# One attention block per pair of graphs in a two-layer graph network: fewer visits to the half-width column tiles of TensorE

## The chip, the core and the metric

The kernel runs on one core of a Trainium2 chip, in float32 throughout. The metric is the time of one execution in microseconds (us), the median of several runs. The core has five engines with an instruction queue each: TensorE (PE in the profile, with its weight loads apart as PEld), VectorE (DVE), ScalarE (ACT), GpSimd (POOL) and SyncE (SP), which only issues DMAs here. TensorE writes to PSUM, which has eight banks of 512 float32 values per partition; the other operands lie in SBUF.

## What is computed

The input is x, 128 graphs of 128 nodes with 512 features, and adj, a 0/1 adjacency for each graph. Two layers follow each other, each with a residual and a normalization over the features:

```python
# layer 0: attention with 8 heads of 64 features
feats = einsum('bnf,hfu->bhnu', X, W)
dense = leaky_relu(e_self[..., :, None] + e_neigh[..., None, :], 0.2) + NEG_BIG * (1 - A)
out   = relu(concat_heads(softmax(dense) @ feats) + b)
x     = layernorm(x + out)
# layer 1: two hypergraph convolutions with the same 128x128 operator R of the graph
h = layer_norm(relu(R @ (x @ W1.T) + b1))          # 1024 features
y = R @ (h @ W2.T) + b2                            # 512 features
x = layernorm(x + (y + x))
```

The softmax is divided out at the end: the heads' features carry a 65th column of ones, so a product of the exponentials with them gives the sum of a row beside its 64 results.

## The kernel before

Graphs are worked on in 64 pairs. Each pair passes through stages that lie in five successive *slots* of the schedule (the lags 0 to 4). In one slot, every stage runs once, each for another pair: while pair p has its attention (lag 2), pair p-1 is in its two convolutions (lag 3), and pair p+1 gets its features (lag 1). The kernel lists all stages with a lag and a time inside the slot, sorts by `time + (p + lag) * T` with T = 38.6, and emits the instructions in this order. The times are thus places in an order, not measured times; each engine then executes its own part of the list strictly in order and waits where data is missing. `at(lag, time, fn, ...)` and `@step(lag, time)` enter a stage; `since` and `until` limit it to some pairs. A few pairs at the start and the last one have an order of their own (`first`, `LAST`).

Products of a pair that share weights are built from seven products with sums of operands in place of eight (`chain`): "pf" for the features of layer 0, "ph" for the first convolution, "py" for the second. A chain takes three PSUM banks, X, Y and W. The product numbered 1 opens bank X, a ScalarE copy (L332) takes the bank's contents away, then products 6, 7 and 4 add to it, with further copies between. GpSimd makes the operand sums ahead of it (`x_sums` and `h_sums` at L458, `z_sums` at L785), VectorE or ScalarE add up the results (`f_sum` L499, `h_sum` L812, `y_sum` L881).

The attention, lag 2:
- exponentials are written to DRAM and read back in blocks, and transposed on VectorE (`e_transpose` L630) into `eT`;
- `attend` (L667) multiplies, for a graph g and a half q of its heads, each head's 128x128 exponentials with its 128x65 features, in two parts of 64 output rows. A part uses half of TensorE's columns, a column tile, and two such parts can be in the array together. Each call takes a PSUM bank (`pav`); both calls of graph 0 lie together, and both of graph 1 some 5 us later, with a feature product and the first "py" product between;
- `attended` (L681, L682, VectorE) divides by the 65th column into `y`;
- `add_bias` (L691, GpSimd), `residual` (L698, VectorE; relu and adding x), `moments` (L706, L707, VectorE), `rstds` (L712 VectorE, L714 GpSimd; the result is rsa), then `first_shift` and `first_output` (L732, L739, ScalarE) finish the normalization.

In the next slot `propagate` (L762, TensorE) multiplies the finished `y` with R into the banks pz, `z_evict` (L774, ScalarE) copies these to zT, and the "ph" chain starts on zT (L797) while GpSimd makes its sums zS (L785). Later in the slot, ScalarE squares h, GpSimd folds the squares (`squares` L850, three levels per graph), and `sum_blocks` (L896 to L901, VectorE) reduces them for the variance; the rest goes over DRAM (`write_sums`, `read_sums`).

PSUM banks are handed out in turn: the ninth request gets the first bank again, once all who read it are done.

Of the kernel before, what the change touches and what calls it, by code (L numbers as in the profile page):

```python
# [8 lines left out]
F32 = mybir.dt.float32  # L9
AF = mybir.ActivationFunctionType  # L10
ALU = mybir.AluOpType
# [9 lines left out]
def kernel(  # L21
# [45 lines left out]
    nc = tc.nc  # L67
    G, N, F = x.shape
    P = 128
    DH = w1t.shape[1]  # L70
    H = 8
    U = F // H
# [11 lines left out]
    work = ctx.enter_context(tc.tile_pool(name="work", bufs=1))  # L84
    small = ctx.enter_context(tc.tile_pool(name="small", bufs=4))
# [3 lines left out]
    def bank(name):  # L89
        return psum.tile([P, HALF], F32, tag="bank", name=name)  # L90
# [109 lines left out]
    for i in range(2):  # L200
        t = const.tile([P, 2, H, UW + 1], F32, name=f"ft{i}")
# [99 lines left out]
    LAST = PAIRS - 1  # L301
    steps = []

    def step(lag, time, since=0, until=PAIRS):

        def keep(fn):
            steps.append((lag, time, fn.__name__, range(since, until), fn, ()))
            return fn
        return keep

    def at(lag, time, fn, *args, since=0, until=PAIRS):
        steps.append((lag, time, fn.__name__, range(since, until), fn, args))

    def chain(kind, lag, times, multiply, w, extra=0, since=0, until=PAIRS):

        tag = "chain" if w == HALF else "half"  # L320

        def product(p, s, i):
            where, start = {1: ("X", 1), 2: ("Y", 1), 6: ("X", 0), 5: ("W", 1), 7: ("X", 0),
                            4: ("X", 0), 3: ("W", 0)}[i]
            if start:
                s[kind, where] = bank(f"{kind}{where}_{p}")
            multiply(s, i, s[kind, where], start)

        def copy(p, s, i):
            n = w + (extra if i < 2 else 0)  # L330
            t = s[kind, i] = work.tile([P, HALF if w == HALF else FW], F32, tag=f"{tag}_{i}", name=f"{kind}{i}_{p}")
            nc.scalar.copy(t[:, :n], s[kind, "X"][:, :n])  # L332

        for i, t in zip((1, 2, 6, 5, 7, 4, 3), times):
            at(lag, t, product, i, since=since, until=until)
        for i, t in enumerate(times[7:]):
            at(lag, t, copy, i, since=since, until=until)
# [145 lines left out]
    def feature(s, i, to, start):  # L483
# [4 lines left out]
          feature, FW, since=2)  # L488
# [181 lines left out]
                )  # L670

    for (g, q), t in (((0, 0), 20.65), ((0, 1), 20.7), ((1, 0), 25.95), ((1, 1), 26.8)):
        at(2, t, attend, g, q)

    def attended(p, s, g):
        if g == 0:
# [7 lines left out]
                t[:, :, :U], rden[:, q, :].unsqueeze(2).to_broadcast([P, HH, U]), op=ALU.mult,  # L684
            )

    at(2, 22.5, attended, 0)
    at(2, 27.9, attended, 1)

    def add_bias(p, s, g):  # L690
        nc.gpsimd.tensor_tensor(s["y"][:, g, :], s["y"][:, g, :], b0_bc, op=ALU.add)  # L691

    at(2, 24.1, add_bias, 0)
    at(2, 29.2, add_bias, 1)

    def residual(p, s, g):
        y = s["y"][:, g, :]
# [21 lines left out]
            op1=ALU.mult,  # L719
        )  # L720

    at(2, 26.2, residual, 0)
    at(2, 30.7, residual, 1)
    at(2, 30.8, rstds, "a")

# [140 lines left out]
    def weigh(s, i, to, start):  # L866
        rows_product(s, i, halves(s["h"], KH // 2), s["hS"], w2_sb, QU, KH // 2, 1, to, start)

    chain("py", 3, (24.2, 29.4, 27.7, 32.9, 31.2, 35.35, 37.1, 26.2, 29.6, 33.1), weigh,
          QU, 1, until=LAST)  # L870

    def y_sum(p, s, g, j, i, where):
# [16 lines left out]

    @step(3, 30.3, until=LAST - 1)
    def sum_blocks(p, s):

        t = s["sq"][:, :, 1, :].rearrange("p g (c f) -> p g c f", c=NB)
        nc.vector.transpose(t, s["sq"][:, :, 0, :].rearrange("p g (c n) -> p g c n", c=NB))  # L896
        nc.vector.tensor_reduce(
            sums_in[:, :2 * NB].rearrange("p (c g) -> p g c", g=2), t, AX.X, ALU.add
        )
        s["sr"] = work.tile([P, B], F32, tag="sr", name=f"sr_{p}")  # L900
        nc.vector.transpose(s["sr"], sums_in)  # L901

    @step(3, 30.32, until=LAST - 1)
    def write_sums(p, s):
        s["sd"] = dram.tile([NB, B, B], F32, tag="sd", name=f"sd_{p}")
        nc.sync.dma_start(s["sd"].rearrange("b q n -> (b q) n"), s["sr"])
# [311 lines left out]
```

## Time and profile before

| | |
|---|---|
| time, median of 3 runs | 2462.02 us (2461.99 to 2462.17) |
| span of the profiled run | 2459.7 us, TensorE clock 0.997 of full |
| busy: PE, PEld | 2427.1 us (99%), 2149.0 us (87%) |
| busy: DVE, ACT, POOL | 2023.0 us (82%), 1532.1 us (62%), 1828.1 us (74%) |
| attention products (L667), 4096 matmuls | 147.9 us busy |
| VectorE's division (L682), 256 | 108.6 us busy, 424 ns each |
| GpSimd's bias (L691), 128 | 162.9 us busy, 1273 ns each |
| GpSimd's squares (L850), 384 | 343.5 us busy, 895 ns each on average |
| VectorE's residual (L698), 128 | 154.4 us busy, 1206 ns each on average |

"Busy" counts an engine's instructions as they lie in time; an instruction that is held up inside the engine counts as busy too, so a mean can hide two kinds of durations. The program writes a float32 matmul as two instructions, which is why 4096 matmuls stand for 2048 products. The page's part 4 follows the work that ended last back through the program, at each step to what released it; the "waits" list names who waited for whom; the "timeline" shows an engine's instructions in order with start and duration, and in brackets the idle time before one.

### The profile page before, as it was taken

How to read it: one execution, taken by the hardware profiler on the slowest of the kernel's cores; microseconds unless marked ns; L12 is line 12 of the kernel's file. 1: busy time of each engine (PE TensorE's matmuls, PEld its weight loads, DVE VectorE, ACT ScalarE, POOL GpSimd, SP SyncE). 2: the span in 40 equal slices, each digit the busy share in tenths (PEclk: the TensorE clock that was granted, in tenths of full speed). 3: DMA queues.
4: the chain of work that ended last, by engine and by line, in shares of the span. 5: the costliest groups of instructions: out<-in, count | busy, mean ns of one | idle time of the engine just before them, and what ended most of it. 6: DMA issues, size and time to landing. Idle time of an engine off the chain costs nothing.

```text
span 2459.7 us, 53018 instructions
## 1 busy us (share of the span) xinstructions
PE 2427.1 (99%) x18273; PEld 2149.0 (87%) x18273; DVE 2023.0 (82%) x4580; ACT 1532.1 (62%) x4481; POOL 1828.1 (74%) x2060
## 2 busy tenths in 40 slices
PE   7999999999999999999999999999999999999998
PEld 5888888888888888888888888888888888888897
DVE  7988888888888888888888888888888888888876
ACT  4665665765756656657557566566575675665763
POOL 5877777777787777777777777778778777777774
PEclk9999999999999999999999999999999999999999
DMA  6545445445455454454454554554545545545531
GB/s 183 143 140 145 145 133 156 141 131 152 138 139 145 141 144 145 132 156 140 129 152 139 143 145 143 146 144 129 153 141 132 152 139 143 143 141 147 145 110 52
DMA packets 432763, 345.30 MB, mean 140 GB/s; under 512 B 153176, under 2 KB 382064, under 8 KB 432496
## 3 DMA queue, kind: packets, MB, share of 16 engines
q1 hardware_dynamic: 429024, 337.46, 48.5%
q10 hardware_dynamic: 3472, 4.47, 0.6%
q8 instruction: 145, 2.38, 0.4%
q14 instruction: 122, 1.00, 0.1%
HBM read 239.08 MB, written 102.73 MB: 139 GB/s over the span
## 4 chain that ended last, share of the span: by engine, by line
PE 50%; DVE 19%; POOL 19%; ACT 6%; issue 3%; DMA 2%; SPq 0%; POOLq 0%; ACTq 0%; DVEq 0%
PE phX L797 10%; PE pyX L476 9%; POOL hS L458 6%; PE pfX L476 5%; PE phW L797 5%; PE pyW L476 5%; POOL zS L785 4%; POOL sq L850 3%; ACT nb L595 3%; PE pav L667 3%; DVE y L953 3%; PE pz L762 2%; PE phY L797 2%; PE pq L963 2%; PE pfW L476 2%
## 5 line engine op out<-in xcount | busy, mean ns | idle before, releaser
L797 PEld LDWEIGHTS phX<-zS,w_sb 128*128 128x128 f32 x3072 | 363.1, 192 | 32.4 <-issue 31.0
L332 ACT COPY py<-pyX 128x257 f32<-128x257 f32 x189 | 70.7, 374 | 506.9 <-PE pyX L476 504.3
L797 PE MATMUL phX<-zS,w_sb 128*128 128x128 f32 x3072 | 374.3, 275 | 1.7 <-POOL xS L458 1.2
L850 POOL TENSOR_TENSOR sq<-sq 128x512 f32<-128x512 f32 (+2 forms) x384 | 343.5, 895 | 20.1
L579 POOL TENSOR_TENSOR nb<-nb,neg 128x512 f32<-128x512 f32 x256 | 318.7, 1279 | 7.6 <-DMA nb<-rd 7.6
L609 ACT ACTIVATE nb<-nb,nm 128x128 f32<-128x128 f32 x1024 | 317.6, 391 | 8.3 <-DVE nm L601 8.3
L595 ACT ACTIVATE nb<-nb,ft 128x128 f32<-128x128 f32 x1020 | 317.2, 389 | 7.5 <-POOL nb L579 7.5
L714 POOL TENSOR_TENSOR rso<-veo,mhalf 128x2 f32<-128x2 f32 x63 | 44.2, 702 | 371.2 <-DVE veo L712 371.2
L827 ACT ACTIVATE h<-h,vecs 128x128 f32<-128x128 f32 x768 | 245.0, 392 | 54.9 <-DVE h L812 54.9
L601 DVE TENSOR_REDUCE nm<-nb 128x4 f32<-128x512 f32 x256 | 174.6, 683 | 111.4 <-ACT nb L595 98.3
L476 PE MATMUL pyX<-w_sb,hS 128*128 128x257 f32 x1008 | 245.6, 385 | 0.0
L476 PE MATMUL pyX<-w_sb,h 128*128 128x257 f32 x1008 | 239.4, 379 | 0.5 <-ACT py L332 0.5
L476 PE MATMUL pyW<-w_sb,hS 128*128 128x256 f32 x1008 | 238.6, 378 | 1.0 <-DVE y L881 1.0
L476 PEld LDWEIGHTS pyW<-w_sb,hS 128*128 128x128 f32 x1008 | 190.7, 189 | 28.7 <-POOL rsa L714 1.4
L476 PEld LDWEIGHTS pyX<-w_sb,hS 128*128 128x128 f32 x1008 | 185.7, 189 | 28.7
L476 PEld LDWEIGHTS pyX<-w_sb,h 128*128 128x128 f32 x1008 | 186.4, 190 | 25.5 <-ACT py L332 0.9
L691 POOL TENSOR_TENSOR y<-y,b_bc 128x512 f32<-128x512 f32 x128 | 162.9, 1273 | 60.4 <-DVE y L682 60.4
L698 DVE SCALAR_TENSOR_TENSOR y<-y,x 128x512 f32<-128x512 f32 x128 | 154.4, 1206 | 56.8 <-POOL y L691 55.1
L667 PEld LDWEIGHTS pav<-ft,eT 128*64 128x64 f32 x4096 | 130.0, 137 | 44.3 <-issue 41.9
L953 DVE SCALAR_TENSOR_TENSOR y<-y,rsh,bw_bc 128x512 f32<-128x512 f32 x126 | 148.6, 1218 | 21.1 <-POOL rsh L949 18.1
L630 DVE STREAM_TRANSPOSE eT<-eb 128x512 f32<-128x512 f32 x252 | 163.5, 687 | 0.9 <-DMA eb<-ed 0.8
L838 ACT ACTIVATE sq<-h 128x512 f32<-128x512 f32 x256 | 160.6, 628 | 2.1
(174 smaller groups left out, 5750.5 us busy)
## 6 DMA issues: line engine op xcount, KB each, us to landing
nb<-rd SPq DMA_DIRECT2D x127, 512.0 KB
ed<-nb SPq DMA_DIRECT2D x126, 512.0 KB
eb<-ed SPq DMA_DIRECT2D x504, 128.0 KB
x<-in_x_dram SPq DMA_DIRECT2D x64, 512.0 KB
out_dram<-o SPq DMA_DIRECT2D x63, 512.0 KB
xb<-in_x_dram SPq DMA_DIRECT2D x248, 128.0 KB
a<-in_adj_dram SPq DMA_DIRECT2D x64, 128.0 KB
w<-in_adj_dram SPq DMA_DIRECT2D x128, 64.0 KB
```

The lines of the kernel that those rows point to most:

```text
L476: nc.tensor.matmul(to[:, :n], lhs[:, k, :], rhs[:, k, :n], start=bool(start) and k == 0, stop=(k == nk - 1), skip_group_check=True,)
L579: nc.gpsimd.tensor_tensor(t, t, neg[:, :, None, :].to_broadcast([P, NB, HH, B]), op=ALU.add)
L595: nc.scalar.activation(t, t, AF.Prelu, bias=s["ft"][:, g, h, 0:1], alpha=SLOPE)
L601: nc.vector.tensor_reduce(s["nm"][:, g, hs], scores(p, s, g, hs).rearrange("p b h j -> p h b j"), AX.XY, ALU.max, negate=True,)
L609: nc.scalar.activation(t, t, AF.Exp, bias=s["nm"][:, g, h:h + 1])
L630: nc.vector.transpose(s["eT"][:, g, hs, :].rearrange("p h (b i) -> p h b i", b=NB), s["eb", g][:, :, hs, :].rearrange("p b h j -> p h b j"),)
L667: nc.tensor.matmul(t[rows, h * (U + 1):(h + 1) * (U + 1)], s["eT"][:, g, q * HH + h, rows], s["ft"][:, g, q * HH + h, 2:], start=True, sto ...
L691: nc.gpsimd.tensor_tensor(s["y"][:, g, :], s["y"][:, g, :], b0_bc, op=ALU.add)
L797: nc.tensor.matmul(to[:, m * N:(m + 1) * N], w[:, k, m * P:(m + 1) * P], rhs[:, k, :], start=bool(start) and m == 0 and k == 0, stop=(k == ...
L827: nc.scalar.activation(dst[:, k, :], src[:, k, :], AF.Relu, bias=b1_sb[:, c:c + 1])
L850: nc.gpsimd.tensor_tensor(t[:, :n, :], t[:, :n, :], t[:, n:2 * n, :], op=ALU.add)
L953: nc.vector.scalar_tensor_tensor(t, t, s["rs", "h"][:, g:g + 1], bw_bc.rearrange("p (j c) -> p j c", j=2), op0=ALU.mult, op1=ALU.add,)
```

## The change

From pair 1 to the last but one, the four `attend` calls become one block that holds both graphs. It uses three banks: seven heads of graph 0, seven heads of graph 1 (7 x 65 = 455 columns each), and one bank for the eighth head of both. The division is done in three steps in place of four, the shared bank first. The block stands at 24.1, where the first "py" product stood; that product moves ahead to 21.0 and its copy to 23.0. The bank of the eighth heads is taken at 20.9, ahead of that product. What follows the attention moves too: on GpSimd, the bias of graph 0 goes from 24.1 to 28.05, which is behind the squares of graph 1 (26.0, 27.3, 28.0), and the bias of graph 1 right behind it to 28.1; on VectorE, graph 0's residual goes from 26.2 to 29.0, and `sum_blocks` from 30.3 to 28.9. The purpose is that TensorE changes to the half-width tiles and back once for a pair instead of twice. The first and the last pair keep the old form.

```diff
-        at(2, t, attend, g, q)
+        at(2, t, attend, g, q, until=1)
+        at(2, t, attend, g, q, since=LAST)
+
+    HB = H - 1
+
+    @step(2, 20.9, since=1, until=LAST)
+    def attend_rest(p, s):
+        s["pav", 2] = bank(f"pav_{p}_2")
+
+    @step(2, 24.1, since=1, until=LAST)
+    def attend_pair(p, s):
+
+        rest = s["pav", 2][:, :2 * (U + 1)].rearrange("p (g u) -> p g u", g=2)
+        to = [(rest[:, g, :], g, HB) for g in range(2)]
+        for g in range(2):
+            t = s["pav", g] = bank(f"pav_{p}_{g}")
+            to += [(t[:, h * (U + 1):(h + 1) * (U + 1)], g, h) for h in range(HB)]
+        for t, g, h in to:
+            for c in range(2):
+                rows = slice(c * P // 2, (c + 1) * P // 2)
+                nc.tensor.matmul(
+                    t[rows], s["eT"][:, g, h, rows], s["ft"][:, g, h, 2:], start=True, stop=True,
+                )
...
-    at(2, 22.5, attended, 0)
-    at(2, 27.9, attended, 1)
+    for g, t in enumerate((22.5, 27.9)):
+        at(2, t, attended, g, until=1)
+        at(2, t, attended, g, since=LAST)
+
+    @step(2, 26.3, since=1, until=LAST)
+    def attended_pair(p, s):
+        y = s["y"] = work.tile([P, 2, F], F32, tag="y", name=f"y_{p}")
+        rden = small.tile([P, 2, H], F32, tag="rden2", name=f"rden_{p}", bufs=2)
+        heads = y.rearrange("p g (h u) -> p g h u", h=H)
+        rest = s["pav", 2][:, :2 * (U + 1)].rearrange("p (g u) -> p g u", g=2)
+        for r, t, dst in [(rden[:, :, HB], rest, heads[:, :, HB, :])] + [
+            (rden[:, g, :HB],
+             s["pav", g][:, :HB * (U + 1)].rearrange("p (h u) -> p h u", h=HB),
+             heads[:, g, :HB, :]) for g in range(2)
+        ]:
+            nc.vector.reciprocal(r, t[:, :, U])
+            nc.vector.tensor_tensor(
+                dst, t[:, :, :U], r.unsqueeze(2).to_broadcast(list(dst.shape)), op=ALU.mult
+            )
...
-    at(2, 24.1, add_bias, 0)
-    at(2, 29.2, add_bias, 1)
+    for g, t in enumerate((24.1, 29.2)):
+        at(2, t, add_bias, g, until=1)
+        at(2, 28.05 + 0.05 * g, add_bias, g, since=1, until=LAST)
+        at(2, t, add_bias, g, since=LAST)
...
-    at(2, 26.2, residual, 0)
+    at(2, 26.2, residual, 0, until=1)
+    at(2, 29.0, residual, 0, since=1, until=LAST)
+    at(2, 26.2, residual, 0, since=LAST)
     at(2, 30.7, residual, 1)
...
-    chain("py", 3, (24.2, 29.4, 27.7, 32.9, 31.2, 35.35, 37.1, 26.2, 29.6, 33.1), weigh,
+    chain("py", 3, (21.0, 29.4, 27.7, 32.9, 31.2, 35.35, 37.1, 23.0, 29.6, 33.1), weigh,
           QU, 1, until=LAST)
...
-    @step(3, 30.3, until=LAST - 1)
+    @step(3, 28.9, until=LAST - 1)
     def sum_blocks(p, s):
...
-    @step(3, 30.32, until=LAST - 1)
+    @step(3, 28.92, until=LAST - 1)
     def write_sums(p, s):
```

## The prediction

> **What bounds the kernel now.** I read the page's shares first, then the chain of work that ended last, the waits, and the timelines of single engines through one slot of the schedule (a slot is the 37.6 us in which every stage runs once, for different pairs). TensorE is busy 99% of the span, so the obvious reading is that only TensorE's instructions count. The page's chain says otherwise:
>
> ```profile
> PE 50%; DVE 19%; POOL 19%; ACT 6%; issue 3%; DMA 2%; SPq 0%; POOLq 0%; ACTq 0%; DVEq 0%
> ```
>
> Only half of the chain is TensorE. The chain in order of time shows which half (start, duration, what):
>
> ```profile
> 1180.54 0.71 POOL rsa L714
> ...
> 1185.77 0.49 ACT zT L774
> 1186.25 0.04 issue
> 1186.30 2.05 PE phX L797 x16
> ...
> 1222.17 1.80 PE pz L762 x16
> 1223.97 0.02 issue
> 1223.99 0.59 ACT zT L774
> 1224.59 0.07 issue
> 1224.66 0.74 POOL zS L785
> ```
>
> It runs through the other engines (POOL, DVE, ACT) for one slot, down to the copy of zT, enters TensorE at the first phX matmul, stays there for one slot to pz, and leaves by zT again. The waits agree:
>
> ```profile
> PEld phX L797 <- ACT zT L774: 10.5, 31, 0.9
> ```
>
> In 31 of 63 slots TensorE stops at phX for zT. The starts of pz show the rhythm: 1184.22 to 1222.01 is 37.79 us (with the stop), 1222.01 to 1259.45 is 37.44 us (without), and 23 slots from 808.05 to 1673.42 average 37.62. So three loops compete. TensorE alone: 37.44 us. The others alone: from the end of the second zT copy to the end of rsa is 31.90 us in each slot that I measured, from there to the first zT copy's end 5.00, to the second's 0.53, together 37.43. And the mixed loop, one slot of each with the stop between: 75.23 us for two, 37.62 each. The mixed loop is the longest and sets the time. A saving on TensorE counts half, and a lengthening of the 31.90 counts half until the loop without TensorE is the longest, then wholly.
>
> What fills the end of the 31.90 us. GpSimd:
>
> ```profile
> 1208.38 1.27 POOL L458 TENSOR_TENSOR hS<-h,hS 128x512 f32<-128x512 f32 x1
> 1209.61 1.28 POOL L691 TENSOR_TENSOR y<-y,b_bc 128x512 f32<-128x512 f32 x1
> 1210.85 2.93 POOL L850 TENSOR_TENSOR sq<-sq 128x512 f32<-128x512 f32 x3
> 1214.76 1.27 POOL L691 TENSOR_TENSOR y<-y,b_bc 128x512 f32<-128x512 f32 x1 [0.98 <-DVE y L682]
> ```
>
> VectorE beside it:
>
> ```profile
> 1210.92 1.74 DVE L698 SCALAR_TENSOR_TENSOR y<-y,x 128x512 f32<-128x512 f32 x1 [0.37 <-POOL y L691]
> ...
> 1214.26 0.42 DVE L682 TENSOR_TENSOR y<-pav,rden 128x256 f32<-128x256 f32 x1
> ...
> 1216.07 0.69 DVE L698 SCALAR_TENSOR_TENSOR y<-y,x 128x512 f32<-128x512 f32 x1
> ```
>
> GpSimd works without a pause from rso (1201.07) to 1213.79. The path is: bias of graph 0, its residual, its statistics, division of graph 1, bias of graph 1, residual of graph 1 at 1216.07. The first residual takes 1.74 us, the second 0.69: the first begins just after GpSimd's squares did (1210.85) and ends 0.55 us after the first of these ended (1212.12). Of the 128 residuals 63 take about 1.74, the others about 0.69: graph 0 pays this in every slot.
>
> TensorE around one visit to the half-width column tiles:
>
> ```profile
> 1204.19 1.05 PE L476 MATMUL pfX<-w_sb,xS 128*128 128x264 f32 x4
> 1205.17 1.15 PE L667 MATMUL pav<-ft,eT 128*64 128x65 f32 x32
> 1206.25 1.16 PE L476 MATMUL pfX<-w_sb,xT 128*128 128x264 f32 x4
> 1207.25 1.05 PE L476 MATMUL pfW<-w_sb,xS 128*128 128x264 f32 x4
> ```
>
> **What the Trainium skill says.** "TensorEngine Tiling (Array Packing)", Key Properties: changing the tiling mode, as against the tile, drains TensorE. The trace agrees: a visit costs what is worked out below as 0.34 us beyond its matmuls. "TensorE: Matmul & The Clock Gate", Part 3: The mechanism: matmuls on different tiles of the array overlap. It agrees: two matmuls of a visit start 7 ns apart, and the next two 58 ns later. "SBUF — State Buffer", SBUF: two separate sides: VectorE with two SBUF inputs and GpSimd reading SBUF share one port pair, an exclusive lock held for the whole instruction, and whichever starts first keeps it. It agrees: 1.74 against 0.69 us above.
>
> **The change part by part.**
>
> TensorE. Four full-width matmuls start 0.89 us apart from the next four (1206.25 is late, 1207.25 to 1208.14 is not). Around the visit: 1204.19 to 1205.17 is 0.98 (0.09 too long), the visit of 32 matmuls, 16 twos at 58 ns, would be 0.93 and with its first gap and its exit is 1.08 (0.15), and 1206.25 to 1207.25 is 1.00 (0.11). That is 0.34 to 0.35 us a visit. One block of 64 in place of two of 32 leaves out one visit: 37.44 becomes 37.10. The matmuls themselves are the same in number. The product of the second convolution at 21.0 has its h long ready; its copy (ACT, 0.37) is hidden by two products and the block, where it had one visit before. The last product of pf comes 0.45 us later, since 1.73 us of pyX now stand before it and 1.08 of attention no longer do, less one switch. So the transpose of x starts at about 1209.5, much as before.
>
> VectorE's division: four reciprocals of 0.16 and four products of 0.42, 2.33 us, become three and three. From 256 columns at 0.42 and 512 at 0.66 (L812) a column costs 0.94 ns, so 448 columns 0.60 and 128 columns 0.30: 2.0 us. It follows x's transpose, 1210.6 to 1212.6, with graph 0 done by 1211.85. TensorE's block runs from 1208.7 to 1210.6, so VectorE doesn't wait there.
>
> GpSimd, which decides. From 1209.61 on: the squares first, now without a residual beside them. Their undisturbed cost is that of the other graph's three, 2.75 us, to 1212.36. Then bias 0 to 1213.59 (1.27, overlapping 0.04), bias 1 to 1214.82. The blocks' sums on VectorE (1.13 us) are done at about 1213.65 and hidden under bias 0. Then residual 0 asks for the port pair. Bias 1, which has no wait left and follows bias 0 on the same engine, has held it since 1213.55, as the squares do before. So the residual ends 0.55 after bias 1, at 1215.37. Statistics 0.03 + 0.70 + 0.03 + 0.18 to 1216.31; then the sum y2 (L881, 0.38, overlapping 0.09), which was hidden and isn't now, to 1216.60; residual 1 at 1216.63. Before it was 1216.07: 0.56 us later.
>
> From residual 1 to zT nothing is changed: ACT idles before rsa (0.79) and works through from it, and the waits of VectorE for the sums' DMA get shorter because these are written 2 us sooner. The eight banks: 17 allocations a slot in place of 18, and each is handed on 6 us or more after its last reader, except pyX's to phX: its last reader stands ahead of zT's copy on ACT, and phX waits for that copy anyway. This costs nothing.
>
> Sum: TensorE alone 37.10, mixed (75.23 − 0.34 + 0.56)/2 = 37.73, without TensorE 37.43 + 0.56 = 37.99. The last wins: 0.37 a slot over 37.62, times 62 slots, 23 us: 2485. TensorE then stops in every slot, and its saving is worth nothing.
>
> **The rivals.** (A) Residual 0 gets the pair ahead of bias 1. Then it is over at 1214.34, bias 1 at about 1215.6, residual 1 starts near 1215.65, 0.42 sooner than now: mixed loop 37.24, 0.38 less, 24 us: 2438. This is what the edit aims at, nearly TensorE's own gain of 21. For it: the saving on TensorE is certain. Against: graph 0's residual lost this race in each of the 63 slots. (B) The path comes out even, by a sum that gives way or a wait that I count twice: mixed loop 37.45, 11 us: 2451. (C) Bias 0 waits for the whole division, not for its own graph: 0.25 later still, 38.24, 38 us: 2500. Against it: phX starts at 1186.30, 0.5 us before the second half of zT is there, so waits go by parts of a tile. (D) No change: gains and losses would have to meet.
>
> **How the numbers follow.** Forecast 0.65; A 0.12; B 0.07; C 0.12; D 0.04. The forecast's own spread is the squares (0.06), the position of residual 0 and the sum (0.1 each): 0.45 to 0.7 a slot, 2478 to 2494. The range takes in C and ends at B: 2451 to 2502, leaving out A, part of B and a little above. Faster 0.19, same 0.05, slower 0.76.
>
> **What would show it.** Right: pz to pz 38.0 us in every slot, no more alternation; phX waiting for zT in some 60 slots, about 0.8 us each; one pav group of 64 a slot; bias 0 and bias 1 back to back on GpSimd; both residual kinds still 1.7 and 0.7. Chain: TensorE well below 50%. Wrong: a first residual of 0.7 us (A), or bias 0 starting on VectorE's last product (C), or phX without waits, in which case the loops are not as I drew them.

## Result and profile after

The changed kernel takes 2470.59 us against 2462.01 before: 8.6 us slower, ratio 1.0036 with a 95% interval of 1.0018 to 1.0053. The forecast was 23 us slower. So the direction and, as the traces show, the mechanism were right, and the size was 2.7 times too large. The traces themselves are of runs 7.4 us apart (spans of 2467.1 and 2459.7).

The page's chain, then two lines of the waits (engine and line, what it waited for: us in total, times, longest):

```profile
PE 55%; DVE 14%; ACT 11%; DMA 11%; POOL 5%; issue 4%; SPq 2%; DVEq 0%; POOLq 0%; ACTq 0%
```

```profile
PEld phX L840 <- ACT zT L817: 37.7, 61, 0.9
...
PEld pav L693 <- issue: 21.4, 62, 0.3
```

TensorE visits the column tiles 62 times in the wait list where it was 124, and it now stops at phX in 61 slots where it was 31. The starts of pz are 37.72 us apart in nearly every slot (23 slots from 811.08 to 1678.72: 37.72 on average, against 37.62 before); the alternation of 37.79 and 37.44 is gone. Sixty-two times 0.10 is 6 us of the difference. From the first pz to the fourth, where the stages start up, 1.1 us is added (119.36 against 118.28), and a few single slots take 37.8 to 37.9 us.

GpSimd and VectorE in the part that decided the forecast:

```profile
1213.93 2.63 POOL L893 TENSOR_TENSOR sq<-sq 128x512 f32<-128x512 f32 x3
1216.51 2.50 POOL L730 TENSOR_TENSOR y<-y,b_bc 128x512 f32<-128x512 f32 x2
1220.90 0.57 POOL L984 TENSOR_TENSOR m<-y 128x1 f32<-128x1 f32 x1 [1.88 <-DVE y L924]
```

```profile
1217.84 0.21 DVE L944 STREAM_TRANSPOSE sr<-sums_in 128x32 f32<-128x32 f32 x1
1217.97 1.59 DVE L739 SCALAR_TENSOR_TENSOR y<-y,x 128x512 f32<-128x512 f32 x1
...
1220.42 0.39 DVE L924 TENSOR_TENSOR y<-py,pyY 128x257 f32<-128x257 f32 x1
1220.73 0.69 DVE L739 SCALAR_TENSOR_TENSOR y<-y,x 128x512 f32<-128x512 f32 x1
```

The order is the one forecast: squares, both biases back to back (1216.51 to 1219.01). Graph 0's residual begins at 1217.97, when the blocks' sums are through on VectorE and the second bias is running, and ends at 1219.56, which is 0.55 us after the second bias. Then GpSimd has nothing to do for 1.88 us.

A warning on the chain: in this slot it runs through the transpose of x, the division, `sum_blocks` and then 6.41 us of a DMA of the sums; such pieces make 4 of the 11 points of the page's "DMA 11%". The next instruction in it, ScalarE's `first_output` (L782), doesn't read these sums, and ScalarE isn't idle ahead of it:

```profile
1223.39 0.48 ACT L775 ACTIVATE sh<-nmean,rsa 128x1 f32<-128x1 f32 x2 [0.79 <-POOL rsa L755]
1223.77 1.51 ACT L782 ACTIVATE y<-y,sh,rsa 128x512 f32<-128x512 f32 x2
```

Its last wait was for rsa, so the chain's step to the DMA is a false one, and its shares can't be used to choose between the loops. The experiments below show which reading holds.

### The profile page after: what moved, and what is told of

It reads as the page before. It is cut to its first block, busy times and chain, and to the rows that moved or that the text cites. A ratio compares the mean times of both kernels' runs of the same rounds, so it can differ in the third digit from the quotient of the medians.

```text
span 2467.1 us, 52770 instructions
## 1 busy us (share of the span) xinstructions
PE 2411.5 (98%) x18273; PEld 2148.6 (87%) x18273; DVE 1997.5 (81%) x4456; ACT 1529.3 (62%) x4481; POOL 1797.7 (73%) x2060
## 4 chain that ended last, share of the span: by engine, by line
PE 55%; DVE 14%; ACT 11%; DMA 11%; POOL 5%; issue 4%; SPq 2%; DVEq 0%; POOLq 0%; ACTq 0%
PE phX L840 17%; PE phW L840 8%; PE pfX L476 8%; ACT nb L595 6%; PE pyX L476 4%; PE phY L840 4%; PE pfW L476 4%; DMA sd<-sr 4%; PE pq L1006 4%; DMA nb<-rd 3%; DVE y L725 3%; ACT y L782 2%; DVE xT L373 2%; DVE y L739 2%; PE pfY L476 2%
## 5 line engine op out<-in xcount | busy, mean ns | idle before, releaser
L893 POOL TENSOR_TENSOR sq<-sq 128x512 f32<-128x512 f32 (+2 forms) x384 | 324.0, 844 | 20.4 <-ACT sq L881 0.3
L499 DVE TENSOR_TENSOR ft<-pf,pfW 128x264 f32<-128x264 f32 x124 | 53.2, 429 | 165.8 <-PE pfW L476 90.1
L458 POOL TENSOR_TENSOR hS<-h 128x512 f32<-128x512 f32 x126 | 158.9, 1281 | 2.3 <-ACT h L870 2.3
L840 PE MATMUL phX<-zT,w_sb 128*128 128x128 f32 x1024 | 131.1, 281 | 26.1 <-ACT zT L817 26.1
```

The costliest lines, as they stand in the source:

```text
L458: engine.tensor_tensor(t[:, i], in0, in1, op=op)
L840: nc.tensor.matmul(to[:, m * N:(m + 1) * N], w[:, k, m * P:(m + 1) * P], rhs[:, k, :], start=bool(start) and m == 0 and k == 0, stop=(k == ...
L893: nc.gpsimd.tensor_tensor(t[:, :n, :], t[:, :n, :], t[:, n:2 * n, :], op=ALU.add)
```

## Experiments

My theory: the loop through GpSimd, VectorE and ScalarE sets the slot, because the second bias takes the port pair (the one that VectorE and GpSimd share) ahead of graph 0's residual; TensorE has slack. Rivals: TensorE's feature product, now later, holds VectorE up (the chain's reading); or the merged block doesn't save TensorE what it seemed to.

**What TensorE alone costs.** Two kernels leave out the attention's bias addition on GpSimd for pairs 1 to 62, to take the other loop out of the way: before, and changed.

```diff
-        at(2, 28.05 + 0.05 * g, add_bias, g, since=1, until=LAST)
```

For the kernel before without it: 

> The kernel before without the same bias additions (it leaves them out for pairs 1 to 62). My theory: no stop at phX is left, every slot is TensorE's 37.44 us: 2451 within 3 us. The difference to the changed kernel without them is what one visit to the column tiles costs TensorE, 0.34 us x 62 = 21 us if it is as read from the starts of the matmuls. Rival (the stops at phX don't come from the bias, residual and normalization): 2462.

For the changed kernel without it: 

> The changed kernel without GpSimd's addition of the attention's bias for pairs 1 to 62 (it leaves that addition out). My theory: with 2.5 us less on GpSimd's path the loop through the other engines falls below TensorE's, which is 37.10 us with one visit, or stays just at the mixed loop of 37.2: 2430 to 2437. Rival (other engines are bound elsewhere, or TensorE's saving isn't 0.34 us): above 2445.

Measured: 2451.2 us (ratio to before 0.9958, 0.9945 to 0.9972) and 2433.5 (0.9888, 0.9874 to 0.9901). pz follows pz after 37.44 us in each slot of the one and after 37.09 in nearly all of the other. So a visit to the column tiles costs TensorE 0.35 us, as read from the starts of the matmuls (the 17.7 us between the totals are less than 62 times that, because a few slots of the changed one are longer, 37.28 to 37.95 us, and it starts up more slowly), and the merging does what it is for. In the chain of the second one TensorE has 94%.

**The saving taken back.** The block cut in two, the eighth heads of both graphs and graph 0 in the first part and graph 1 in the second, with the propagator's four matmuls between:

```diff
-    @step(1, 34.7)
+    @step(1, 24.12)
     def propagator(p, s):
...
-    @step(2, 24.1, since=1, until=LAST)
-    def attend_pair(p, s):
...
+    def attend_part(p, s, g):
...
+    at(2, 24.1, attend_part, 0, since=1, until=LAST)
+    at(2, 24.14, attend_part, 1, since=1, until=LAST)
```

> The changed kernel with the attention block cut in two again, the propagator's four matmuls moved between the halves, so that TensorE visits the column tiles twice per pair. All else stays. My theory (TensorE has slack in every slot of the changed kernel and waits 0.6 us for zT): the 0.34 us come out of this wait, which falls to about 0.25 us, and the time stays at 2470.6 within 4 us. Rival (TensorE's part is on the path, because its feature product releases VectorE or because the chain is half TensorE): 0.17 to 0.34 us a slot more, 2481 to 2492.

Measured: 2474.3 us (1.0051, 1.0037 to 1.0065), 3.7 over the changed kernel, with intervals that overlap. A slot takes 37.78 us (median) where it was 37.72. The wait of phX for zT fell from 37.7 us in 61 slots to 18.8 in 60, so nearly all of TensorE's 0.34 us came out of it. The 0.06 that is left fits the mixed loop: with the 0.35 us by which graph 1's residual is late (it starts 29.62 us after the end of the second copy of zT, where it was 29.28), it is (75.23 + 0.35) / 2 = 37.79, just above the other, and the slots alternate again a little (37.84 and 37.70). I had left that loop out of this expectation, and no run tests this reading apart. The first slot is 2.0 us longer too (45.27 against 43.31); why stays open.

**The port pair.** One GpSimd instruction moved between the two biases, the mask of a later pair, 0.41 us:

```diff
-    @step(0, 30.63)
+    @step(0, 30.63, until=3)
     def mask(p, s):
...
+    at(0, 28.07, mask, since=3)
```

> The changed kernel with GpSimd's 0.41 us mask moved from after the attention's stages to between the two bias additions, nothing else. My theory (GpSimd's second bias addition takes the shared port pair just ahead of graph 0's residual, and the loop through the other engines sets the time): the residual waits for the mask only and ends about 0.85 us sooner, its duration falls from 1.6 to about 0.9; the second bias then waits for it; graph 1's residual starts 0.8 us sooner; a slot falls from 37.72 to about 37.2 us, the time from 2470.6 to about 2440 (2432 to 2450), below the kernel before. Rival (TensorE's late feature product holds the transpose of x, the division and the blocks' sums ahead of the residual, as the profile's chain of after has it): the residual can't start sooner and its end hardly matters, the time stays within 3 us of 2470.

Measured: 2446.7 us (0.9938, 0.9925 to 0.9950): 24 us less than the changed kernel and 15 less than before. GpSimd and VectorE in one slot, with the mask first:

```profile
1394.37 1.27 POOL L732 TENSOR_TENSOR y<-y,b_bc 128x512 f32<-128x512 f32 x1
1395.73 0.40 POOL L366 TENSOR_SCALAR neg<-a 128x256 f32<-128x256 f32 x1
1396.10 1.70 POOL L732 TENSOR_TENSOR y<-y,b_bc 128x512 f32<-128x512 f32 x1
```

```profile
1395.79 0.88 DVE L741 SCALAR_TENSOR_TENSOR y<-y,x 128x512 f32<-128x512 f32 x1
```

Here the residual ends 0.54 us after the mask and not after a bias, and it is now the second bias that is held: 1.70 us in place of 1.27. This is the order that I had expected, but only 12 of 58 slots have it. In the other 46 the residual comes ahead of the mask too, and it is the mask that is held, 0.90 us in place of 0.40:

```profile
1358.66 0.90 POOL L366 TENSOR_SCALAR neg<-a 128x256 f32<-128x256 f32 x1
```

```profile
1358.61 0.69 DVE L741 SCALAR_TENSOR_TENSOR y<-y,x 128x512 f32<-128x512 f32 x1
```

Graph 1's residual starts 0.71 us sooner than in the changed kernel (median). The slots take 37.28 us on average, near what was expected (37.2); some alternate again, 37.44 and 37.09, others lie at 37.2 to 37.3. The total is 7 us over the centre of what I expected, of which 3.5 us is the first slot (46.78 us, in the changed kernel 43.31), where the mask of pair 3 now waits 2.70 us for its adjacency between the two biases. The rival that reads the chain by its letter is out: nothing on TensorE, the transpose, the division or the DMA was touched.

The same edit on the kernel before, from pair 4 on, at 24.15, between graph 0's bias and graph 1's squares:

> The kernel before with GpSimd's mask moved to stand between graph 0's bias and graph 1's squares, from pair 4 on; no merging of the attention. My theory: graph 0's residual then waits for 0.4 us of mask at most instead of 1.27 us of squares and ends about 0.85 us sooner; the squares lose up to 0.5 us to it, so graph 1's bias and residual come 0.5 us sooner; the loop through the other engines falls to 36.9 us, the mixed loop to 37.4, and TensorE's own 37.44 us is what is left: 2451 (2448 to 2455), the time of the kernel before without any bias. Rival (the order on the shared port matters only with the merged block): 2462.

Measured: 2455.5 us (0.9971, 0.9961 to 0.9982), half a microsecond above the expected range. The slots are 37.56 and 37.45. The residual won over the mask in all of 58 slots, took its 0.69 us, and the mask was held (0.91 us). Graph 1's bias came 0.35 us sooner and its residual only 0.2, not 0.5: `sum_blocks` and the sum y2, which stand in front of it on VectorE, come after graph 1's squares. Part of the time is to be had without merging anything.

**What the reordering behind the block is worth.** The merged block with what follows it in the order of before:

```diff
-    @step(2, 26.3, since=1, until=LAST)
+    @step(2, 25.85, since=1, until=LAST)
     def attended_pair(p, s):
...
-        at(2, 28.05 + 0.05 * g, add_bias, g, since=1, until=LAST)
+        at(2, (25.9, 29.2)[g], add_bias, g, since=1, until=LAST)
...
-    at(2, 29.0, residual, 0, since=1, until=LAST)
+    at(2, 26.2, residual, 0, since=1, until=LAST)
```

with `sum_blocks` and `write_sums` back at 30.3 and 30.32. 

> The changed kernel with the merged block, but what follows it in the order of the kernel before: division at once, graph 0's bias ahead of the squares, graph 0's residual right after it, the blocks' sums back at 30.3. My theory: GpSimd idles from the end of the operand sums until the block has given graph 0 (about 1.3 us), then graph 1's bias comes behind squares that the residual slows; graph 1's residual starts 0.3 us later than in the changed kernel; 38.05 us a slot, 2489 (2482 to 2500). Rival (the new order behind the block is what costs the time): below 2466.

Measured: 2485.6 us (1.0093, 1.0078 to 1.0109), 37.96 us a slot.

```profile
1223.63 1.27 POOL L730 TENSOR_TENSOR y<-y,b_bc 128x512 f32<-128x512 f32 x1 [1.44 <-DVE y L725]
1224.85 2.94 POOL L893 TENSOR_TENSOR sq<-sq 128x512 f32<-128x512 f32 x3
```

GpSimd idles for 1.44 us until the late block has delivered graph 0. So the change's new order isn't what costs the time; it gives back 15 us of the 24 that the later block takes.

**The product ahead, undone alone.**

```diff
-    chain("py", 3, (21.0, 29.4, 27.7, 32.9, 31.2, 35.35, 37.1, 23.0, 29.6, 33.1), weigh,
+    chain("py", 3, (23.6, 29.4, 27.7, 32.9, 31.2, 35.35, 37.1, 25.5, 29.6, 33.1), weigh,
```

> The changed kernel with the first product of the second convolution back behind the feature products, so that nothing stands between the feature chain's third X product and the one that waits for its copy. My theory: TensorE stops about 0.6 us there for ScalarE's copy; through the mixed loop half of it counts, so 37.9 us a slot, about 2482 (2474 to 2488). Rival (TensorE's wait for zT takes it all up, as TensorE has slack): 2470. Second rival (the earlier feature product lets VectorE's division start sooner, and this sets the time): below 2466.

Measured: 2485.6 us (1.0092, 1.0079 to 1.0106). The waits show a new stop of TensorE in 62 slots, where the feature product waits for ScalarE's copy:

```profile
PEld pfX L476 <- ACT pf L332: 54.8, 62, 0.9
...
PEld phX L840 <- ACT zT L817: 7.2, 30, 0.9
```

VectorE's division starts 0.9 us sooner here (its first product 23.14 us after zT, not 24.05; as above, counted from the end of the second copy, over all slots), and graph 1's residual starts at the same place, 29.62 us after zT, in both. That is the cleanest evidence that TensorE's later feature product isn't on the path. It settles one thing more. In the changed kernel `sum_blocks` on VectorE ends a little late, and graph 0's residual begins 0.18 us after its bias, so these sums might be to blame. Here it is ready 0.03 us after the bias, loses to the second bias all the same, and takes 1.74 us. The slots average 37.97, and phX waits for zT in every other one (30), as it did before the change: this is the mixed loop again.

**A version for both limits.** Graph 1's third level of squares goes between the biases in place of the mask, `sum_blocks` (with `write_sums` at 30.83) behind graph 1's statistics, the transpose of x behind the division:

```diff
-            at(3, ((17.0, 17.1, 17.2), (26.0, 27.3, 28.0))[g][level], squares, g, level)
+            at(3, ((17.0, 17.1, 17.2), (26.0, 27.3, 28.07))[g][level], squares, g, level)
...
-    @step(3, 28.9, until=LAST - 1)
+    @step(3, 30.82, until=LAST - 1)
     def sum_blocks(p, s):
...
-    at(0, 26.15, x_transpose, 0, since=2)
+    at(0, 26.35, x_transpose, 0, since=2)
```

> The changed kernel reordered for both limits: graph 1's last level of squares (0.45 us) between the two biases, so that graph 0's residual waits for this and not for graph 1's bias; the transpose of x behind the division; the blocks' sums behind graph 1's statistics. My theory: graph 1's residual starts about 1.2 us sooner than in the changed kernel (0.86 sooner than before), the loop through the other engines and the mixed loop fall below TensorE's 37.10 us, and TensorE sets the time: 2432 to 2438, below all kernels with the full computation so far. Against it: the sums go to DRAM 3 to 4 us later, and if they come back too late, the second normalization and its chain wait: then 2445 or more.

Measured: 2431.8 us (0.9874, 0.9861 to 0.9888), just below the expected range and 31 us below the kernel before, with the whole computation. pz follows pz after 37.09 us in 58 of 63 slots, TensorE's own loop, and no wait of phX for zT is left in the list.

```profile
1198.60 1.28 POOL L730 TENSOR_TENSOR y<-y,b_bc 128x512 f32<-128x512 f32 x1
1199.83 0.47 POOL L893 TENSOR_TENSOR sq<-sq 128x128 f32<-128x128 f32 x1
1200.24 1.73 POOL L730 TENSOR_TENSOR y<-y,b_bc 128x512 f32<-128x512 f32 x1
```

```profile
1199.91 0.93 DVE L739 SCALAR_TENSOR_TENSOR y<-y,x 128x512 f32<-128x512 f32 x1 [0.62 <-POOL y L730]
```

```profile
PE 97%; DVE 2%; POOL 1%; issue 0%; DMA 0%; ACT 0%; POOLq 0%; DVEq 0%; SPq 0%; ACTq 0%
```

The sums that go to DRAM later did no harm. Which of the three edits is worth how much wasn't tried one by one.

## Why the prediction was right and wrong

Right: that half of the chain wasn't TensorE and that three loops compete; TensorE's loop of 37.10 us (37.09 measured); that the stops at phX would come in every slot and eat the saving; the order on GpSimd and who gets the port pair; that the bias starts on its own graph's part of the division (it starts 25.41 us after zT, graph 1's division ends at 25.88), which excludes rival C. Rival A was lost in the changed kernel. Once something stood between the biases, its slot came nearly true (37.28 us for 37.24), its total not (2446.7 for 2438).

Wrong: the term "37.43 + 0.56 = 37.99", the loop without TensorE. It measured 37.72: 32.24 us from the second copy of zT to the end of rsa, where 31.90 + 0.56 was forecast, then 5.00 and 0.48. Three entries of it were too large. The squares: I took the other graph's 2.75 us,

```profile
1201.74 2.75 POOL L850 TENSOR_TENSOR sq<-sq 128x512 f32<-128x512 f32 x3
```

and these take 2.63, so the first bias starts 2.59 us after the squares begin and not 2.71: 0.12. The stretch from the end of graph 0's residual to the start of graph 1's: 1.17 us, not 1.26, since the residual behind the sum overlaps it by 0.07 us where I had put 0.03 between them: 0.09. And the second copy of zT: 0.48 us behind the first, not 0.53, when nothing holds it: 0.05. Together 0.26 of the 0.27 us; the rest is rounding. So graph 1's residual is 0.35 us late, not 0.56.

An error of 0.27 us in 38 would be nothing, but the forecast was the distance of this loop from the slot of before, 37.62, and that fell from 0.37 to 0.10. I gave it a spread of 0.45 to 0.7 us of lateness, which left out what happened; the range held only thanks to the rivals. That the direction held is luck in part: 0.10 us was left of it, and the error was 0.27. The 1.1 us of the start-up had no place in the forecast.

Two signs failed with it: the stops at phX are 0.6 us each (37.7 us in 61), not 0.8, and TensorE's share of the chain rose to 55% in place of falling well below 50%; as shown above, this chain takes a false step through a DMA. And one statement was wrong without a part in the sum: VectorE's waits for the sums' DMA were to get shorter, as these are written 2.0 us sooner. They grew from 9.8 us in 16 waits to 39.2 in 34; the read that follows the write is issued 1.1 us later than before.

The undisturbed squares could have been had from the trace level by level (1.26, 0.79, 0.46 and two gaps of 0.08), which gives 2.67; in the changed kernel the levels take 1.29, 0.73 and 0.45.

## What to carry to other kernels

An engine that is busy 99% of the time can still be half of the chain: where two slots alternate in length, look for a second loop, and price a saving in each loop before summing. Merging work on the busiest engine made its consumers later here, and the order behind it on the other engines was worth more (24 us for one moved mask) than the saving itself (17.7 us between the two kernels without the bias). Where two engines share a port, put a short instruction of the one between two long ones at the place where the other asks.

## What was not expected of the hardware

GpSimd's second `tensor_tensor` starts about 0.04 us before the first ends and so is ahead of a VectorE instruction that the first one releases (0.03 us after its end in the kernel before). A `tensor_scalar` behind a `tensor_tensor` on GpSimd starts 0.08 us after its end, and with the mask in that place the residual mostly came first: its median was 0.69 us, and the mask was held, 0.90 us with the merged block and 0.91 without. The Trainium skill's "SBUF — State Buffer", SBUF: two separate sides, says that whichever starts first keeps the pair; in these runs differences of about 0.05 us decide it. The starts that the profile records don't tell by themselves who has the pair: in 5 slots of the changed kernel with the mask between, the mask is recorded from 0.08 us after the bias and the residual only from 0.09 to 0.13, and still the residual went through in 0.65 us while the mask was held for 0.92 to 0.96. From 0.14 us on, in 12 slots, the mask came first.
